# Side pieces of a state-space scan queued by an account of engine work, with depthwise taps as diagonal products on TensorE

## The chip, the cores and the metric

The kernel runs on one core of one Trainium2 chip. It uses TensorE (PE: matrix products into PSUM, with its weight load PEld), VectorE (DVE), ScalarE (ACT), GpSimd (POOL) and SyncE (SP, which here only issues DMAs). The metric is the device time of one execution in microseconds (us); lower is better. All tensors are float32.

## The reference

One layer works on x of shape (4, 256, 32, 32): four batches, 256 channels, 1024 tokens. Cut to what matters:

```python
xs = layernorm_over_channels(x)                      # twice, with and without weights
xc = xn split in 4 groups of 64 channels
xm = mamba(xc) + skip * xc                           # per group: u, z = xs @ inw.T; causal conv of 4 taps; silu;
                                                     # dt = softplus(...); h = exp(dt*A) * h + dt*u*B; y = sum_s h*C
g  = sigmoid(pointwise(grouped_conv3(xm)));  xg = g * xm
R   = pointwise(depthwise3(xg, rdw_w)) + xg
cat = concat(xs, R)
xm2 = pointwise(depthwise3(cat, fdw_w)) + xs
x_local, x_global = depthwise3(xm2, lc_w), mha(xm2)  # 8 heads of 32
xo = gelu(layernorm(concat(x_local, x_global) @ fc_w.T))
xi = depthwise3x3(ln_hw(xo), dwc_w)                  # 9 taps per channel on the 32 x 32 image
x  = x + proj(layernorm(xi))
t  = tokens of x;  t = t + top-2-of-8 experts(layernorm(t))   # 256 -> 1024 -> 256
```

## The kernel before, in words

Channels lie on the 128 partitions (two chunks `c` of 256 channels), tokens along the free dimension, in two halves `h` of 512. For each batch `b` there are eight *parts*: group `n` = 0 to 3, half `h` = 0 and 1; so parts 0, 2, 4, 6 are first halves and parts 1, 3, 5, 7 second halves. A part has 16 *steps*; a step scans 128 of the 128 x 16 pairs of channel and state, 32 channels x 4 states on the partitions.

`scan` writes the instructions of a step. In `step`, VectorE makes dBu (line 528) and scans it along 512 tokens (line 535); GpSimd keeps the last column in first halves (line 539) and multiplies by C (line 540). ScalarE makes the decay dA three steps ahead (line 521). TensorE makes the B rows of the next four steps (`spread_b`, line 513) and sums states of the last four (`sums_of`, line 546), each as four products on a quarter of the array. Tables `before`, `behind` and `group` say at which step the pieces of the part before, the part behind and the next group are written: state sums at step 1, `gather` at 3, `project_out` at 6, `add_skip` at 8.

The order of instructions on every engine is the order in which the program writes them (`manual_schedule`). All the rest of the layer is written as generators, the *side pieces*: `normalised` (layer norm of the next batch), `convolutions` (gate, three-tap convolutions, pointwise products, then values, queries and keys in `prepared`), `attention`, `local`, and `mixing` (output projection, `fc`, norm, GELU, the 3x3 convolution, norm, projection, then `dispatch`, which routes tokens to experts and scatters 16 row blocks with indirect DMAs, line 1423). After each step `beat` advances a clock by one, and each running generator, in the order of the list `running`, runs until its own due time lies ahead: `yield 1` means due again at the next beat, `yield 2` at the one after, `yield 0` now. `drain` beats without scans until no generator is left. `in_turn` writes a product for one item and, two items later, the use of an earlier one.

The program starts `convolutions(b-1)` at part 0 of batch b. It waits until step 9 of that part, when the batch's scans have all been gathered. After part 3 `drain` is called, then attention(b-1), with mixing(b-1) behind it, local(b-1) and normalised(b+1) are started; beats run without scans until the attention is nearly through; then parts 4 to 7 follow, with mixing beside them, and what is left of mixing and its `dispatch` goes on beside the next batch's part 0. The last batch's convolutions, attention and mixing run with no scan beside them.

A three-tap depthwise convolution (`depthwise3`) is one activation on ScalarE for the first tap (line 353) and two instructions on VectorE that multiply by a column of weights and add (line 358), each on 128 x 1024. The 3x3 one in `mixing` is an activation for the middle tap (line 1013) and eight such instructions per chunk (line 1021). `product` (line 325) is a pointwise convolution: chunks of 128 x 128 weights on 512 tokens. In the profile one float32 product shows as two records of matmul and two of weight load.

After the layer the routed tokens go through the experts in 39 tiles (lines 1510 to 1578), and the result is brought back.

Of the kernel before, what the change touches and what calls it, by code (L numbers as in the profile page):

```python
# [1 line left out]

# [7 lines left out]
F32 = mybir.dt.float32  # L10
# [4 lines left out]
P = 128  # L15
# [29 lines left out]

LOG_EXP = "natural_log_exp_and_others"


# [18 lines left out]
def network(  # L67
# [26 lines left out]
):  # L94
    nc = tc.nc
    shifted = sums is None
# [18 lines left out]
    def col(name, i=0, rows=slice(0, P)):  # L115
# [3 lines left out]
    ident = cpool.tile([P, P], F32, name="ident")  # L119
    make_identity(nc, ident)  # L120
    ones_mean = cpool.tile([P, P], F32, name="ones_mean")
# [12 lines left out]
        W1, W2, b2, out,  # L134
    )


    with tc.tile_pool(name="w_conv", bufs=1) as wp, tc.tile_pool(
# [88 lines left out]

        ones = wp.tile([P, P], F32, name="ones")
        nc.gpsimd.memset(ones, 1.0)

# [90 lines left out]
        def product(name, w, co, chunks):  # L321

            out = ps(name)
            for ci, chunk in enumerate(chunks):
                nc.tensor.matmul(
                    out, w[:, ci, ts(co, P)], chunk, start=(ci == 0), stop=(ci == len(chunks) - 1)
                )
            return out

        def column_mean(name, chunks):  # L330

            out = ps(name)
            for ci, chunk in enumerate(chunks):
                nc.tensor.matmul(
                    out, ones_mean, chunk, start=(ci == 0), stop=(ci == len(chunks) - 1)
                )
            return out

        def in_turn(items, make, use, lag=2):

            made = []
            for at in range(len(items) + lag):
                if at >= lag:
                    use(items[at - lag], made[at - lag])
                if at < len(items):
                    made.append(make(items[at]))
                yield 1
# [3 lines left out]
        def depthwise3(dst, c, src, c_src, w, wi, bias):  # L351

            nc.scalar.activation(
                dst[:, c, :], src[:, c_src, 0:N], AF.Identity, bias=bias, scale=col(w, 3 * wi)
            )
            yield 1
            for k in (1, 2):
                nc.vector.scalar_tensor_tensor(
                    dst[:, c, :], src[:, c_src, k : k + N], col(w, 3 * wi + k), dst[:, c, :],
                    ALU.mult, ALU.add,  # L360
                )
                yield 1

        LEFT = KC - 1
# [8 lines left out]
        def normalised(b):  # L373
# [20 lines left out]
            for h in range(2):  # L394
                sq = [a2(f"sq_{b}_{h}_{c}") for c in range(NC2)]
                for c in range(NC2):
                    nc.gpsimd.tensor_tensor(sq[c], part(c, h), part(c, h), ALU.mult)
                yield 1
                var = column_mean(f"var_{b}_{h}", sq)
                yield 2  # L400
                root(r1[:, half(h)], var, eps6)
                yield 1
                root(r2[:, half(h)], var, eps11, scale=1.0 + 1e-5)
                yield 1
# [104 lines left out]
        def spread_b(b, n, h, q):  # L509
            bs = T[b, n, h, "bs", q] = ps(f"bs_{b}_{n}_{h}_{q}")  # L510
            for i, r in enumerate(states):
                s = DTR + 4 * q + i
                nc.tensor.matmul(  # L513
                    bs[r], xpwT_s[:, n, s : s + 1].to_broadcast([P, 32]),
                    T[b, n, "u"][:, half(h)], start=True, stop=True,
                )
# [25 lines left out]
        def sums_of(b, n, h, q):  # L542
            if q == 0:
                T[b, n, h, "yp"] = ps(f"yp_{b}_{n}_{h}")
            for g in range(GD):
                nc.tensor.matmul(  # L546
                    T[b, n, h, "yp"][ts(g, 32)], quads, T[b, n, h, "hs", q * GD + g],
# [15 lines left out]
        def add_skip(b, n, h):  # L563
# [9 lines left out]
        before = {  # L573
            1: [(sums_of, GS - 1)], 3: [(gather,)], 6: [(project_out,)], 8: [(add_skip,)],
        }
# [44 lines left out]
        def scan(at, i, stop):  # L620
# [17 lines left out]
            if g == 0 and q + 1 < GS:  # L638
                spread_c(b, n, h, q + 1)
            if g == 1 and q > 0:  # L640
                sums_of(b, n, h, q - 1)
# [31 lines left out]
        def convolutions(b):  # L673
# [49 lines left out]
            for c in range(NC2):  # L723
# [3 lines left out]
                yield 1  # L727
            for c in range(NC2):
                yield from depthwise3(d[1], c, xm, c, "rdw_w", c, col("rdw_b", c))

# [11 lines left out]
            d[1] = a8(f"d4r_{b}")  # L742
            for c in range(NC2):
                yield from depthwise3(d[1], c, xm, c, "fdw_w", NC2 + c, col("fdw_b", NC2 + c))

# [84 lines left out]
        def attention(b):  # L830
# [12 lines left out]
            def logits(g, h, kt):  # L843
# [3 lines left out]
                for i in range(4):  # L847
                    r = ts(i, HD)
                    nc.tensor.matmul(  # L849
                        sts[i], k[r, ts(kt, P)], q[r, half(h)], start=True, stop=not shifted  # L850
# [14 lines left out]
            def sum_pair():  # L865
                kt, acc, es = pairs.pop()
                for i in range(4):
                    nc.tensor.matmul(
                        acc[ts(i, HD)], ones[:, 0:HD], es[i], start=(kt == 1), stop=(kt == NK - 1)
                    )  # L870
# [18 lines left out]
            for at, (g, h, kt) in enumerate(steps):  # L889
# [6 lines left out]
                for i in range(4):  # L896
                    nc.tensor.matmul(  # L897
                        accs[0][ts(i, HD)], v8[:, kt, ts(4 * g + i, HD)], es[i],
# [21 lines left out]
            for _ in ending.pop():  # L920
                yield 1

        def local(b):
# [8 lines left out]
        def mixing(b):  # L932
# [25 lines left out]
            def inverse_deviation(name):  # L958
# [8 lines left out]
                for h in range(2):  # L967
                    sq = squares(h)
                    yield 1
                    var = column_mean(f"var_{name}_{h}", sq)  # L970
                    yield 2
# [30 lines left out]
            xi = a8(f"xi_{b}")  # L1002
            xz = []
            for c in range(NC2):
                xz.append(
# [5 lines left out]
                )  # L1011

                nc.scalar.activation(
                    xi[:, c, :], xz[c].rearrange("p i j -> p (i j)"), AF.Identity,
                    bias=col("dwc_b", c), scale=col("dwc_w", 9 * c + 4),
                )
                yield 1
                for k in (0, 1, 2, 3, 5, 6, 7, 8):
                    acc = xi[:, c, :].rearrange("p (i j) -> p i j", j=WW)
                    (to_i, at_i), (to_j, at_j) = (edge(d - 1) for d in divmod(k, 3))  # L1020
                    nc.vector.scalar_tensor_tensor(
                        acc[:, to_i, to_j], xz[c][:, at_i, at_j], col("dwc_w", 9 * c + k),
                        acc[:, to_i, to_j], ALU.mult, ALU.add,
                    )
                    yield 1 if k % 2 else 0

            xc = xi
# [44 lines left out]

        def beat():

            nonlocal tick
            tick += 1
            for one_ in list(running):
                while one_[0] <= tick:
                    try:
                        one_[0] += max(next(one_[1]), 0)  # L1080
                    except StopIteration:
                        running.remove(one_)
                        break

        def drain():
# [11 lines left out]
        with tc.manual_schedule(engines=ALL):  # L1097
            log_exp()
            start(normalised(0), weights())
            drain()  # L1100
            first_part()
            for b in range(B):
                for p in range(PARTS):
# [6 lines left out]
                    for i in range(NSTEP):  # L1110
                        scan(at, i, stop)
                        if b > 0 and p == 0 and i == 9:
                            whole(b - 1)
                        beat()
                    if b > 0 and p == PARTS // 2 - 1:
# [7 lines left out]
                        while not T.get(("attended", b - 1)):  # L1123
                            beat()
                        resume(at + 1)
            start(finish_part(len(parts) - 1))
            drain()
# [33 lines left out]
class Experts:  # L1161
# [141 lines left out]
    def dispatch(self, b, X1, XR, root):  # L1303
# [116 lines left out]
        for j in range(2):  # L1420
            for t in range(NT):
# [8 lines left out]
                self.sent.append(ins)  # L1430
                yield 1

# [267 lines left out]
```

## Time and profile before

| | |
|---|---|
| time before, median of 3 | 2745.61 us (2745.22 to 2754.72) |
| the profiled execution's own time | 2743.95 us |
| its span | 2742.2 us, mean granted clock 0.893 |
| busy PE, PEld | 2179.7 us (79%), 983.5 us (36%) |
| busy DVE, ACT, POOL | 1736.6 (63%), 1164.7 (42%), 1142.1 us (42%) |
| batch 0's scans | 78.2 to 359.8 us |
| batch 1, 2, 3: parts 0 to 3 | 168.5, 190.7, 189.9 us |
| batch 1, 2, 3: attention without scans | 93.6, 92.4, 82.4 us |
| batch 1, 2, 3: parts 4 to 7 | 179.8, 178.9, 177.8 us |
| last batch's rest with no scan | 1713.8 to about 2040 us |
| experts | about 2040 to 2742 us |

The limits of parts are the starts of their first scan at line 535; after part 3 the attention's stretch begins 32.5 us after that part's first scan. A stretch's busy times say which engine was full in it; a busy PE is not PE at its peak, since matmuls are pipelined.

### The profile page before, as it was taken

Reading aid. Unit: us, or ns where it says so; the run is one execution under the profiler, and the core shown is the slowest. Engines: PE = TensorE matmul, PEld = TensorE weight load, DVE = VectorE, ACT = ScalarE, POOL = GpSimd, SP = SyncE. Lnnn points to the kernel's source line nnn. Section 1 sums busy time; section 2 is a strip of 40 time slices with the busy share of each in tenths; the row PEclk is TensorE's granted clock in tenths of the full one; section 3 lists DMA queues with packets and bytes.
Section 4 is the critical chain, followed back from the end, with each engine's and each line's share of the span. In section 5 each row is a group of like instructions: output and inputs, shape, how many; then the busy total and the mean of one; then the engine's idle time right before and its main releaser. Section 6 shows DMA issues by size and latency. Waiting matters only on the chain. (4 is left out here: it accounts for less than half of the span.)

```text
span 2742.2 us, 28466 instructions
## 1 busy us (share of the span) xinstructions
PE 2179.7 (79%) x9082; PEld 983.5 (36%) x9082; DVE 1736.6 (63%) x2413; ACT 1164.7 (42%) x1938; POOL 1142.1 (42%) x1171
## 2 busy tenths in 40 slices
PE   6677787999676899867689976599439998999972
PEld 2111112322121332212132211232128777777761
DVE  2789989778999887899987889437431211211211
ACT  2544544575554368545347662246312222222220
POOL 2677767425775742676671366300021111111112
PEclk8888988999888999989799997799769999999995
DMA  2434432302242320333321132100056554555526
GB/s 84 110 99 102 100 98 66 82 24 50 68 132 54 97 59 24 77 79 103 82 69 43 30 77 52 62 4 13 0 187 211 181 171 160 179 178 181 180 72 199
DMA packets 148839, 263.26 MB, mean 96 GB/s; under 512 B 28256, under 2 KB 94084, under 8 KB 147656
## 3 DMA queue, kind: packets, MB, share of 16 engines
q1 hardware_dynamic: 136240, 233.68, 29.9%
q0 software_dynamic: 7408, 20.35, 2.1%
q10 hardware_dynamic: 5032, 7.32, 0.8%
q8 instruction: 73, 1.20, 0.2%
q14 instruction: 86, 0.70, 0.1%
HBM read 159.39 MB, written 34.77 MB: 71 GB/s over the span
## 5 line engine op out<-in xcount | busy, mean ns | idle before, releaser
L540 POOL TENSOR_TENSOR hs<-hs,cs 128x512 f32<-128x512 f32 x512 | 689.2, 1347 | 205.0 <-DVE hs L535 154.5
L521 ACT ACTIVATE dA<-dts,A 128x512 f32<-128x512 f32 x512 | 343.0, 713 | 299.6 <-DMA dts<-dt 197.6
L546 PE MATMUL yp<-hs,quads 128*32 128x512 f32 x1024 | 315.4, 675 | 154.2 <-POOL hs L540 126.8
L528 DVE TENSOR_TENSOR dBu<-dts,bs 128x512 f32<-128x512 f32 x512 | 347.9, 680 | 41.5 <-DMA dts<-dt 24.2
L1559 ACT ACTIVATE hs<-h,b 128x256 f32<-128x256 f32 x312 | 147.9, 474 | 470.5 <-PE h L1555 470.5
L535 DVE TENSOR_TENSOR_SCAN hs<-dA,last,dBu 128x512 f32<-128x512 f32 x256 | 327.6, 1280 | 24.9 <-ACT sq_fin L964 0.5
L535 DVE TENSOR_TENSOR_SCAN hs<-dA,dBu 128x512 f32<-128x512 f32 x256 | 312.4, 1220 | 30.7 <-ACT dA L521 6.7
L1555 PE MATMUL h<-xT,w 128*128 128x256 f32 x1248 | 285.1, 387 | 43.8 <-DVE xT L1536 43.8
L1574 POOL DMA_INDIRECT Y<-ys,dest x78 | 74.6, 957 | 559.6 <-DVE ys L1573 367.7
L859 ACT ACTIVATE e<-st 128x512 f32<-128x512 f32 x512 | 264.8, 603 | 89.6 <-PE st L849 88.8
L1563 PE MATMUL y<-w,hs 128*128 128x256 f32 x1248 | 275.9, 379 | 0.0
L1555 PEld LDWEIGHTS h<-xT,w 128*128 128x128 f32 x1248 | 229.9, 192 | 92.6 <-DVE xT L1536 53.3
L1563 PEld LDWEIGHTS y<-w,hs 128*128 128x128 f32 x1248 | 237.1, 190 | 32.2
L513 PE MATMUL bs<-u,xpwT_s 128*32 128x512 f32 x1024 | 175.3, 676 | 60.1 <-DVE hs L535 50.7
L539 POOL COPY last<-hs 128x1 f32<-128x1 f32 x256 | 92.4, 361 | 299.9 <-DVE hs L535 292.7
L909 DVE TENSOR_TENSOR e<-e,e 128x512 f32<-128x512 f32 x256 | 167.1, 714 | 51.3 <-ACT e L859 26.7
L546 PEld LDWEIGHTS yp<-hs,quads 128*32 128x32 f32 x1024 | 51.8, 117 | 392.3 <-POOL hs L540 287.9
L849 PE MATMUL st<-qk 32*128 32x512 f32 x1024 | 173.9, 651 | 4.4 <-DVE hs L535 4.1
L1529 DVE TENSOR_REDUCE b<-mine 128x8 f32<-128x64 f32 x39 | 8.5, 219 | 263.5 <-ACT hs L1559 263.5
L430 PE MATMUL up<-xn,inwk 64*128 64x512 f32 x256 | 138.5, 688 | 26.3 <-DVE hs L535 19.6
L897 PE MATMUL av<-e,v 128*32 128x512 f32 x1024 | 142.1, 615 | 0.0
L1539 DVE TENSOR_SCALAR late<-xs,expert 128x2 f32<-128x2 f32 x39 | 8.9, 228 | 201.5 <-DMA xs<-XS 201.5
(267 smaller groups left out, 2679.9 us busy)
## 6 DMA issues: line engine op xcount, KB each, us to landing
w<-in_W_dram SPq DMA_DIRECT2D x78, 1024.0 KB, 5.5
dts<-dt SPq DMA_DIRECT2D x512, 128.0 KB, 2.4
cs<-cd SPq DMA_DIRECT2D x512, 64.0 KB, 2.1
xs<-XS SPq DMA_DIRECT2D x39, 260.0 KB, 5.0
yy<-Y SPq DMA_DIRECT2D x8, 1024.0 KB, 6.5
b<-in_b_dram SPq DMA_DIRECT2D x39, 128.0 KB, 5.0
xn<-in_x_dram SPq DMA_DIRECT2D x4, 1024.0 KB
XL<-xl SPq DMA_DIRECT2D x8, 512.0 KB, 2.8
```

What stands on the lines that cost most here:

```text
L513: nc.tensor.matmul(bs[r], xpwT_s[:, n, s : s + 1].to_broadcast([P, 32]), T[b, n, "u"][:, half(h)], start=True, stop=True,)
L521: nc.scalar.activation(dA, T[b, n, h, "dts", g][:, 0, :], AF.Exp, scale=A[:, g, n, q : q + 1])
L528: nc.vector.tensor_tensor(dBu, T[b, n, h, "dts", g][:, 1, :], T[b, n, h, "bs", q], ALU.mult)
L535: nc.vector.tensor_tensor_scan(hs, T[b, n, h, "dA", i], dBu, 0.0 if h == 0 else last, ALU.mult, ALU.add)
L540: nc.gpsimd.tensor_tensor(hs, hs, T[b, n, h, "cs", q], ALU.mult)
L546: nc.tensor.matmul(T[b, n, h, "yp"][ts(g, 32)], quads, T[b, n, h, "hs", q * GD + g], start=(q == 0), stop=(q == GS - 1),)
L849: nc.tensor.matmul(sts[i], k[r, ts(kt, P)], q[r, half(h)], start=True, stop=not shifted)
L859: nc.scalar.activation(es[i], sts[i], AF.Exp, scale=1.0 / HD**0.5)
L909: nc.vector.tensor_tensor(first[i], first[i], es[i], ALU.add)
L1555: nc.tensor.matmul(hp[:, i, :], w1[:, c, ts(k, P)], xT[:, c, :], start=(c == 0), stop=(c == NC2 - 1),)
L1559: nc.scalar.activation(hs[:, k, :], hp[:, i, :], AF.Gelu, bias=b1_s[:, k, :])
L1563: nc.tensor.matmul(yp[:, ts(t, C)], hs[:, k, ts(t, P)], w2[:, k, :], start=(k == 0), stop=(k == NHC - 1),)
```

## The change

Each engine gets a `Meter`: whenever the program names an instruction of that engine, a fixed price is added to its account. Products on a quarter of the array go to a meter of their own, a quarter of which is charged to TensorE. While scans run, `beat` goes on with side pieces only as long as neither TensorE nor ScalarE nor GpSimd stands more than 1.0 above VectorE's account; an account never falls more than 2.0 below it. The rule holds in all of batch 0, in parts 0 to 3, and after the attention is over; in a drain and while attention runs without scans it does not. `product` and `column_mean` become generators that may be interrupted after each product. The taps of `rdw_w`, of the second half of `fdw_w` and of the 3x3 convolution become TensorE products with diagonal matrices, made by ScalarE; those of the first half of `fdw_w` and of `local` stay as they were. State sums move from step 1 to 2 and from g == 1 to g == 2, `gather` from step 3 to 4, scatters to every second beat. `ones` is the experts' tile of ones.

```diff
+class Meter:
+    def __init__(self, engine, cost):
+        self.engine, self.cost, self.us = engine, cost, 0.0
+
+    def __getattr__(self, name):
+        self.us += self.cost.get(name, 0.0)
+        return getattr(self.engine, name)
...
+        self.vector = Meter(nc.vector, {
+            "tensor_tensor": 0.7, "tensor_tensor_scan": 1.25, "scalar_tensor_tensor": 1.0,
+            "tensor_copy": 0.2, "tensor_scalar": 0.3, "tensor_reduce": 0.3, "bn_stats": 0.6,
+            "bn_aggr": 0.2, "reciprocal": 0.2,
+        })
+        self.scalar = Meter(nc.scalar, {"activation": 0.7, "copy": 0.6})
+        self.gpsimd = Meter(nc.gpsimd, {
+            "tensor_tensor": 1.4, "tensor_scalar": 2.0, "tensor_copy": 0.35,
+            "indirect_dma_start": 1.0,
+        })
+        self.tensor = Meter(nc.tensor, {"matmul": 0.86, "transpose": 0.25})
+        self.quarter = Meter(nc.tensor, {"matmul": 0.86})
...
-    nc = tc.nc
+    nc = Metered(tc.nc)
...
+    experts.nc = nc
...
-        ones = wp.tile([P, P], F32, name="ones")
-        nc.gpsimd.memset(ones, 1.0)
+        ones = experts.every
...
                     out, w[:, ci, ts(co, P)], chunk, start=(ci == 0), stop=(ci == len(chunks) - 1)
                 )
+                yield 0
             return out
...
+        def depthwise3_pe(name, dst, src, w, at, bias):
+            diags = []
+            def diagonals(c):
+                for k in range(3):
+                    diags.append(small.tile([P, P], F32, tag="diag", name=f"dg_{name}_{c}_{k}", bufs=4))
+                    nc.scalar.activation(
+                        diags[-1], ident, AF.Copy, scale=col(w, 3 * (at + c) + k)
+                    )
+            def taps(item):
+                c, h = item
+                out = ps(f"{name}_{c}_{h}")
+                for k in range(3):
+                    nc.tensor.matmul(
+                        out, diags[3 * c + k], src[:, c, ds(k + h * HALF, HALF)],
+                        start=(k == 0), stop=(k == 2),
+                    )
+                if item == (0, 1):
+                    diagonals(1)
+                return out
+            diagonals(0)
+            yield 1
+            yield from in_turn(
+                CO_H, taps,
+                lambda item, out: nc.scalar.activation(
+                    dst[:, item[0], half(item[1])], out, AF.Identity, bias=col(bias, at + item[0])
+                ),
+            )
...
         before = {
-            1: [(sums_of, GS - 1)], 3: [(gather,)], 6: [(project_out,)], 8: [(add_skip,)],
+            2: [(sums_of, GS - 1)], 4: [(gather,)], 6: [(project_out,)], 8: [(add_skip,)],
         }
...
-            if g == 1 and q > 0:
+            if g == 2 and q > 0:
                 sums_of(b, n, h, q - 1)
...
-            for c in range(NC2):
-                yield from depthwise3(d[1], c, xm, c, "rdw_w", c, col("rdw_b", c))
+            yield from depthwise3_pe(f"rd_{b}", d[1], xm, "rdw_w", 0, "rdw_b")
...
-            for c in range(NC2):
-                yield from depthwise3(d[1], c, xm, c, "fdw_w", NC2 + c, col("fdw_b", NC2 + c))
+            yield from depthwise3_pe(f"fd1_{b}", d[1], xm, "fdw_w", NC2, "fdw_b")
...
             for _ in ending.pop():
                 yield 1
+            T["over", b] = True
+            level()
...
+            order = [(c, k) for c in range(NC2) for k in (4, 0, 1, 2, 3, 5, 6, 7, 8)]
+            def taps(at):
+                for c, k in order[at : at + 1]:
+                    if k == 4:
+                        banks[c] = [ps(f"dw_{b}_{c}_{h}") for h in range(2)]
...
+                    for h in range(2):
...
+                        nc.tensor.matmul(
...
+                            diags[c, k], xz[c][:, lo + move : hi + move, at_j],
+                            start=(k == 4), stop=(k == 8),
+                        )
...
-                for k in (0, 1, 2, 3, 5, 6, 7, 8):
-                    acc = xi[:, c, :].rearrange("p (i j) -> p i j", j=WW)
-                    (to_i, at_i), (to_j, at_j) = (edge(d - 1) for d in divmod(k, 3))
-                    nc.vector.scalar_tensor_tensor(
-                        acc[:, to_i, to_j], xz[c][:, at_i, at_j], col("dwc_w", 9 * c + k),
-                        acc[:, to_i, to_j], ALU.mult, ALU.add,
-                    )
-                    yield 1 if k % 2 else 0
+            diagonals(2)
+            for at in range(len(order)):
+                taps(at)
+                diagonals(at + 3)
+                yield 0
+                if at % 9 == 8:
+                    c = at // 9
+                    yield 2
+                    for h in range(2):
+                        nc.scalar.activation(
+                            xi[:, c, half(h)], banks[c][h], AF.Identity, bias=col("dwc_b", c)
+                        )
...
-        def beat():
+        def beat(beside=False):
             nonlocal tick
             tick += 1
+            others = (nc.tensor, nc.scalar, nc.gpsimd)
+            nc.tensor.us += nc.quarter.us / 4
+            nc.quarter.us = 0.0
+            for engine in others:
+                engine.us = max(engine.us, nc.vector.us - 2.0)
             for one_ in list(running):
-                while one_[0] <= tick:
+                while one_[0] <= tick and not (
+                    beside and max(e.us for e in others) > nc.vector.us + 1.0
+                ):
                     try:
                         one_[0] += max(next(one_[1]), 0)
...
+        def level():
+            for engine in (nc.tensor, nc.scalar, nc.gpsimd):
+                engine.us = nc.vector.us
...
-                        beat()
+                        beat(beside=not b or p < PARTS // 2 or T.get(("over", b - 1)))
...
                         resume(at + 1)
+                        level()
...
                 self.sent.append(ins)
-                yield 1
+                yield 2
```

## The prediction, made before the change was run

> **What bounds the kernel now.** I read the 40 slices of the page first, then busy time by stretch, cut at the first scan of each part (DVE line 535), then the groups by form, then the timeline of one crowded part and of the stretch after the last scan. The chain that ended last is no help: it holds only the last 4 us.
>
> ```profile
> PE   6677787999676899867689976599439998999972
> DVE  2789989778999887899987889437431211211211
> PEclk8888988999888999989799997799769999999995
> ```
>
> Up to about 1700 us VectorE (DVE) is nearly full and TensorE is not far behind; then comes a stretch with neither full, and from 2040 us the experts, which the change does not touch. A stretch's columns are length, then busy time of PE, PEld, DVE, ACT, POOL, then clock:
>
> ```profile
> 294.50:326.40 31.90, 26.49 (x88) 6.45 (x88) 30.25 (x34) 18.48 (x27) 26.36 (x36) 0.95 0.42 103
> 326.40:359.80 33.40, 22.98 (x73) 3.98 (x72) 31.47 (x35) 13.91 (x22) 24.21 (x20) 0.93 0.41 99
> ...
> 852.70:908.70 56.00, 32.10 (x100) 8.35 (x98) 54.28 (x67) 21.75 (x31) 40.04 (x43) 0.76 0.28 75
> 908.70:959.90 51.20, 43.06 (x140) 16.54 (x138) 39.89 (x43) 21.93 (x33) 38.14 (x50) 0.93 0.32 85
> 959.90:992.40 32.50, 31.19 (x119) 10.99 (x117) 31.05 (x33) 19.48 (x32) 23.61 (x19) 0.96 0.35 85
> ...
> 1171.00:1225.80 54.80, 35.33 (x85) 9.61 (x81) 53.22 (x57) 22.39 (x31) 42.09 (x35) 0.75 0.28 72
> ```
>
> The first two are parts (16 scan steps) with no side work: three such, 33.1, 31.9 and 33.4, average 32.8 us, nearly all of it dBu and scan. The others carry side pieces of batch 0 or 1. At 1171 (the 3x3 taps) VectorE has 53 of 54.8 us busy; at 908 (pointwise products) it is idle 11 us, of which its residuals wait 9.7 us for line 325's products. So the parts are held by VectorE in one place and by TensorE's order in another.
>
> ```profile
> 1659.41 2.48 DVE L1021 SCALAR_TENSOR_TENSOR xi<-xz,V,xi 128x961 f32<-128x961 f32 x2
> 1660.73 2.29 POOL L540 TENSOR_TENSOR hs<-hs,cs 128x512 f32<-128x512 f32 x1
> 1661.81 0.69 DVE L528 TENSOR_TENSOR dBu<-dts,bs 128x512 f32<-128x512 f32 x1
> 1662.53 1.22 DVE L535 TENSOR_TENSOR_SCAN hs<-dA,dBu 128x512 f32<-128x512 f32 x1
> ```
>
> One step costs 0.69 + 1.22 of VectorE, and two taps beside it 2.48: the taps double the step. (GpSimd's product takes 2.29 beside them, 1.27 alone, but is not last.)
>
> **The taps, one by one.** Removed per batch: 4 + 4 taps of line 358 at 1.26 and 16 of line 1021 at 1.24, 30 us of VectorE. Added: 12 + 12 + 36 products of 512 columns. A product is two records; these rows show its price (first row warm, last row from a cold start), the quarter products' (second) and the 3x3's in the tail:
>
> ```profile
> 1798.88 1.45 PE L325 MATMUL fp<-d4r,fpwT_s 128*128 128x512 f32 x3
> ...
> 1683.03 1.06 PE L513 MATMUL bs<-u,xpwT_s 128*32 128x512 f32 x8
> ...
> 1952.44 20.17 DVE L1021 SCALAR_TENSOR_TENSOR xi<-xz,V,xi 128x961 f32<-128x961 f32 x16 [2.58 <-ACT xi L1013]
> 1972.76 4.68 PE L334 MATMUL mean<-xi,ones_mean 128*128 128x512 f32 x6 [8.00 <-DVE xi L1021]
> 1985.80 9.00 PE L325 MATMUL pr<-xi,projT_s 128*128 128x512 f32 x16 [2.70 <-DVE xi L976]
> ```
>
> Three warm records take 1.45, the last of them 0.59 (the shortest at line 325), so they start 0.43 apart: 0.86 a product, 51.6 us of TensorE per batch for 30 us of VectorE. Diagonals (128x128 on ScalarE) have no row: between 0.21 (128x8, line 1368) and 0.60 (128x512, line 859); I take 0.3, as the shape is nearer the first: 30 of them 9 us (6 to 18), and 12 evictions of 0.69, 8 us, less 6 activations of 1.24: 10 us more a batch (7 to 19) on an engine that is half idle in these stretches, hidden by the three decays queued ahead (6 us of scan); behind a diagonal that waits for its buffer (four, freed by the taps) stand the decays, and for them the scans; if that cover goes, each such wait costs its length. The 3x3 also holds two PSUM banks over nine taps where it held none; with bs two, yp, dBu and up's two, all eight are taken in a first half: between 0 and one step (2 us) each time, I take 0.
>
> **The account.** In what follows "priced" is the diff's own cost table. Per part VectorE is priced 16 x 1.95 + 2 x 1.0 = 33.2. GpSimd is priced 19 x 1.4 = 26.6, and in first halves another 16 x 0.35 = 32.2: headroom 1.0 in a first half, 6.6 in a second. TensorE's own work is 32 quarter products / 4 x 0.86 = 6.9 plus 12 or 4 full ones, 13.8 on average: headroom 19.4, or 22 products a part. A side piece is queued only while all three stand below VectorE + 1.0, and unused headroom beyond 2.0 is lost. From this I can place every piece:
>
> Batch 1, parts 0 to 3 (side: batch 0's convolutions, 96 priced products). From step 9 of part 0 there are 3.4 parts x 22 = 75 products, and 12 side taps and residuals on VectorE are priced 12 us, 14 more, less a few lost in waits: some 11 products are left when part 3 ends, and the drain runs them with no scan beside. 4 x 32.8 + 4 taps 5.1 + 8 residuals 5.9 + residuals behind their products 9 (before: 9.7 in one part) + drain 11 x 0.86 = 9.5: 161 to 164, against 168.5 before. Take -5.
>
> Parts 4 to 7 of batches 1 and 2 (side: end of attention, then mixing with 8 + 16 + 4 + 36 + 4 + 4 + 8 = 80 products, 3.6 parts of headroom). The last mean, variance and projection slip into the next batch's part 0, with xr's load and XD's store on SP; these pass only spreads of dts and cs (2.4 and 2.1 us to landing), among which they stood before: 0. 131 + end blocks 8.4 (39.6 busy less a clean 31.2) + bn and lgn 5 + a wait of 5 for the first inverse deviation, now queued without its spacing + 6 since four quarter products really take 1.06 (line 513) where 0.86 is priced, eight times a part: 156, against 179.8 and 178.9: -24 and -23. This is the gain.
>
> Batches 2 and 3, parts 0 to 3: the step that decides. dispatch's 16 scatters are priced 1.0 each on GpSimd. By the account they start at step 3 of part 1, and what GpSimd has from there is 8 (3 from floor to limit, 13 x 0.55 + 2.0 - 4.2) + 1.0 + 6.6 = 15.6, against 16 scatters and two gate products of 1.4. Mixing stands ahead of convolutions in the list of running pieces, so each bit of headroom goes to a scatter, and the max over engines stops the convolutions too. They stand at the gate from part 1, through two parts with scans alone, until the drain after part 3. There 64 products of 0.86 and 16 of 0.43 (256 columns) run with VectorE idle: 62 us. Time: 131 + leftover centring, scaling and residuals 8 + dispatch 13 + 4 taps 5 + waits 10 + 62 = 229, against 190.7 and 189.9: +38 and +39. The waits: a piece that was held comes due several times over and is queued in one go (mean, squares, variance and root in one beat, where line 970 once waited two); behind the scaling on VectorE stand dBu and scan, and for them GpSimd and TensorE wait. In the tail mean to scaling takes 1984.52 - 1972.76 = 12 us; TensorE runs some 2 us ahead, so I take 10, between 0 and 12.
>
> Parts 4 to 7 of batch 3: mixing finishes inside: 156 + 8 + 9 of such waits = 173, against 177.8: -5. After the last scan dispatch follows as before: 0.
>
> Tail (batch 3, nothing beside): the convolutions were 55 us from line 724 (1769.5) to the first logits (1824.8); now 12 + 8 + 12 + 16 + 16 products and 16 half ones follow one another, 72 x 0.86 = 62, and a first eviction and residual: 64, +9. The 3x3 was 20.2 on VectorE; now 36 x 0.86 = 31.0, +2.0 for a cold start (line 325's 16 records take 9.00, warm ones 15 x 0.43 + 0.59 = 7.0), +1.4 evictions, less about 2 as the mean then finds the array warm: +12. Sum +21.
>
> The Trainium skill's TensorE: Matmul & The Clock Gate (What's actually happening) has the array at half rate until about 3.4 us of sustained work; by it the cold start would be worth half of that, 1.7 us, not 2.0, and the sum 0.3 less.
>
> Sums moved one step later (steps 2 and 4, g == 2) let the TensorE queue stand less behind GpSimd (PE's waits of 126.8 us at line 546), mostly idle time off the path: -2 in batch 0, between -10 and 0. Scatters at every second beat: between -16 (their own 16 x 1.0) and 0; 0, as GpSimd is not last in those parts (38 of 51 busy). ones from the experts' tile: the same matrix, 0.
>
> Sum: -2 - 5 - 24 + 38 - 23 + 39 - 5 + 21 = +39 on 2743.95, the profiled execution's own time (span 2742.2 and 1.75 around it); it lies 1.7 under the median of 2745.61, so 2785. Uncertain are the two drains, the three stretches of parts 4 to 7 and the tail by 8 each, in square 20, and the waits by up to 10 a batch, 30 for three: 36 together.
>
> **Rivals.** *Faster:* the convolutions of batches 1 and 2 do get their turns, so drains stay short. For it: VectorE idles 18 us in those four parts before and loses 10 us of taps. Price: both +38 become -5: 2744 - 2 - 5 - 24 - 5 - 23 - 5 - 5 + 21 = 2696, 2698 at the median. It decides if rd's diagonal products of batch 1 are queued before part 3 of batch 2 ends. Against it: 15.6 of headroom for 18.8. *Much slower:* TensorE becomes the bound in parts 4 to 7, where the account keeps it as full as VectorE while its in-order queue still waits at line 546 for GpSimd: a part takes 39 instead of 35 to 37, the 24 + 23 + 5 us of gain go, 2837. *No change:* gains in parts 4 to 7 of some 36 each cancel the drains, about 2745.
>
> **How the numbers follow.** About 0.5%, 14 us, is what a measurement here can tell. Chances: forecast 0.55, much slower 0.10, no change 0.11, faster 0.24. So slower 0.65, same 0.11, faster 0.24. The range reaches down to 2688, ten under the faster case, and up to the much slower one; the forecast's own range is 2750 to 2820.
>
> **What would show it.** Right: batch 2 and 3's parts 2 and 3 take about 33 us each with almost no line 325, then some 60 us with TensorE full and no line 535; parts 6 of 55 us become about 36; L1021 gone, its time in the tail 31 to 35 us. Wrong: rd products beside scans in batch 2 (then the faster case), or parts 4 to 7 above 39 us (then the much slower one).

## The result and the profile after

The changed kernel takes 2822.47 us (median of 4 runs, 2815.76 to 2835.08) against 2745.41 for the kernel before, timed alternately: a ratio of 1.0283, 95% interval 1.0234 to 1.0331. The forecast was 2785 with a range of 2688 to 2840: the sign and the places were right, the size was 37 us short, and the forecast's own case (2750 to 2820) ended 2 us below what came. The profiled execution took 2815.76 us (span 2814.0), against 2743.95 (2742.2) before.

The 40 slices of its page show two new holes in VectorE (DVE): 5 and 3 tenths in slices 14 and 15 and 2 in slice 22, where it stood at 8, 8 and 7 before, with TensorE (PE) at 7, 9 and 9:

```profile
PE   6767779998978799898679988599747999999982
DVE  2888898689977537997862798418231111121111
PEclk8887789999977799997879999799978999999995
```

Busy time by stretch, columns as before (length, then PE, PEld, DVE, ACT, POOL, clock). The first line is a part 6 of batch 1, the next four are parts 0 to 3 of batch 2, the last the stretch after them, with no scan:

```profile
697.30:734.30 37.00, 31.95 (x99) 11.03 (x99) 32.46 (x39) 22.75 (x38) 25.84 (x35) 0.86 0.33 80
767.40:831.10 63.70, 52.40 (x175) 21.72 (x176) 45.17 (x62) 27.48 (x42) 26.71 (x38) 0.76 0.38 106
831.10:886.30 55.20, 40.51 (x114) 8.64 (x107) 44.54 (x82) 23.30 (x35) 29.51 (x32) 0.75 0.24 61
886.30:926.40 40.10, 33.14 (x88) 8.47 (x89) 30.42 (x35) 18.65 (x28) 30.23 (x42) 0.66 0.38 99
926.40:958.90 32.50, 21.45 (x69) 4.87 (x63) 30.69 (x33) 13.04 (x25) 29.76 (x32) 0.79 0.41 106
958.90:1025.00 66.10, 59.35 (x150) 28.90 (x148) 6.15 (x9) 14.46 (x26) 6.76 (x8) 0.95 0.08 27
```

Part 6, 54.8 us before, is 37.0. Part 3 has nothing beside its scans (32.5), and 66 us of products follow with VectorE at 6 us. Parts 0 and 1 take 63.7 and 55.2 with about 45 us of VectorE each: it is idle for 29 us in the two. The pointwise products of the same stretches (line 359: length, PE, PEld) say who was held. Part 0 has the 16 records of the last projection; in parts 1 to 3 there is none:

```profile
767.40:831.10 63.70, 7.93 (x16) 2.71 (x16) 0.76 0.38 106
831.10:886.30 55.20, 0.00 (x0) 0.00 (x0) 0.75 0.24 61
886.30:926.40 40.10, 0.00 (x0) 0.00 (x0) 0.66 0.38 99
926.40:958.90 32.50, 0.00 (x0) 0.00 (x0) 0.79 0.41 106
958.90:1026.00 67.10, 34.83 (x80) 15.16 (x80) 0.95 0.08 26
```

In the tail the 3x3 is now these products (TensorE's timeline, start and length):

```profile
2017.98 32.01 PE L1094 MATMUL dw<-xz,dg 128*128 128x512 f32 x72 [9.28 <-ACT dg L1081]
2049.83 3.60 PE L369 MATMUL mean<-xi,ones_mean 128*128 128x512 f32 x8
```

By stretch, in the two profiled executions (starts of the first scans; "to part 4" holds the attention's stretch too):

| stretch | before | after | difference | forecast |
|---|---|---|---|---|
| batch 0 | 281.6 | 284.9 | +3 | -2 |
| batch 1, part 0 to part 4 | 262.1 | 251.1 | -11 | -5 |
| batch 1, parts 4 to 7 | 179.8 | 153.1 | -27 | -24 |
| batch 2, part 0 to part 4 | 283.1 | 350.4 | **+67** | **+38** |
| batch 2, parts 4 to 7 | 178.9 | 151.8 | -27 | -23 |
| batch 3, part 0 to part 4 | 272.3 | 340.8 | **+68** | **+39** |
| batch 3, parts 4 to 7 | 177.8 | 160.5 | -17 | -5 |
| last scan to the end | 1028.4 | 1043.1 | +15 | +21 |
| sum | | | +72 | +39 |

### The profile page after: what moved, and what is told of

Its sections match the earlier page's. It is cut to its first block, busy times and chain, and to the rows that moved or that the text cites. A ratio compares the mean times of both kernels' runs of the same rounds, so it can differ in the third digit from the quotient of the medians.

```text
span 2814.0 us, 29508 instructions
## 1 busy us (share of the span) xinstructions
PE 2331.2 (83%) x9562; PEld 1067.1 (38%) x9562; DVE 1590.9 (57%) x2317; ACT 1205.0 (43%) x2082; POOL 1055.4 (38%) x1170
## 5 line engine op out<-in xcount | busy, mean ns | idle before, releaser
L609 POOL TENSOR_TENSOR hs<-hs,cs 128x512 f32<-128x512 f32 x512 | 650.5, 1274 | 221.8 <-DVE hs L604 176.3
L615 PE MATMUL yp<-hs,quads 128*32 128x512 f32 x1024 | 242.7, 690 | 53.1 <-POOL hs L609 48.4
L499 PE MATMUL up<-xn,inwk 64*128 64x512 f32 x256 | 170.6, 824 | 8.1 <-POOL xn L481 6.8
L608 POOL COPY last<-hs 128x1 f32<-128x1 f32 x256 | 51.2, 200 | 321.1 <-DVE hs L604 314.6
L916 PE MATMUL st<-qk 32*128 32x512 f32 x1024 | 163.9, 638 | 0.2
L1094 PE MATMUL dw<-xz,dg 128*128 128x496 f32 (+3 forms) x288 | 135.6, 620 | 14.9 <-ACT dg L1081 14.9
L615 PEld LDWEIGHTS yp<-hs,quads 128*32 128x32 f32 x1024 | 39.5, 117 | 230.8 <-POOL hs L609 127.2
```

The source lines that it names most:

```text
L499: nc.tensor.matmul(up, inwk[rows, c, k, :], XN[b][rows, c, ds(k + h * HALF, HALF)], start=(k == 0), stop=(k == KC - 1),)
L609: nc.gpsimd.tensor_tensor(hs, hs, T[b, n, h, "cs", q], ALU.mult)
L615: nc.quarter.matmul(T[b, n, h, "yp"][ts(g, 32)], quads, T[b, n, h, "hs", q * GD + g], start=(q == 0), stop=(q == GS - 1),)
L916: nc.quarter.matmul(sts[i], k[r, ts(kt, P)], q[r, half(h)], start=True, stop=not shifted)
```

## The experiments

The theory: mixing's last pieces (norm, projection, dispatch) are held by the account and come out bunched in parts 0 and 1; its scatters, priced on GpSimd, then hold the convolutions at the gate's multiplication (line 793) until the drain. Two columns make a quick test of it in each kernel: the time from the first scan of part 0 to that of part 3 of batch 2 (bunching and waits), and from there to part 4 (32.5 us of scans, the drain, then attention).

Medians and ratios are against the kernel before as timed beside each (2744.74 to 2751.99); the stretches are from one profiled execution each.

| kernel | median us | ratio to before, 95% | part 0 to 3 | part 3 to 4 |
|---|---|---|---|---|
| before | 2745.41 | 1 | 158.2 | 124.9 |
| after | 2822.47 | 1.0283 [1.0234, 1.0331] | 159.0 | 191.4 |
| e1, scatters free | 2718.42 | 0.9867 [0.9833, 0.9901] | 159.6 | 136.4 |
| e2, taps alone | 2703.76 | 0.9825 [0.9782, 0.9867] | 151.2 | 124.9 |
| e3, account alone | 2715.45 | 0.9867 [0.9836, 0.9899] | 147.7 | 130.0 |
| e4, e1 and mixing's end not held | 2674.25 | 0.9709 [0.9679, 0.9740] | 143.5 | 134.4 |
| e5, moved steps alone | 2764.67 | 1.0068 [1.0040, 1.0095] | 161.6 | 125.4 |
| e6, e4 with the tail's taps on VectorE | **2657.47** | 0.9665 [0.9636, 0.9694] | 143.6 | 134.3 |
| e7, 3x3 on VectorE | 2775.51 | 1.0106 [1.0075, 1.0136] | 140.4 | 162.1 |
| e8, e6 with the old steps | 2690.49 | 0.9787 [0.9758, 0.9815] | 150.3 | 134.6 |
| e9, after with the old steps | 2819.36 | 1.0266 [1.0239, 1.0293] | 162.1 | 191.6 |
| e10, e4 with scatters priced | 2680.99 | 0.9759 [0.9726, 0.9792] | 142.4 | 134.1 |
| e11, only the 3x3 on TensorE | 2801.91 | 1.0208 [1.0173, 1.0243] | 159.0 | 184.7 |

**e1: the scatters' price.**

```diff
-            "indirect_dma_start": 1.0,
+            "indirect_dma_start": 0.0,
```

> The changed kernel with one number changed: an indirect DMA is priced 0 instead of 1.0 on GpSimd's account. Theory (the scatters eat GpSimd's headroom, so the convolutions are held until the drain): by the account the convolutions of batches 1 and 2 then run beside parts 1 to 3 as batch 0's do, and 11 instead of 80 products are left for each drain; the stretches of 66 us between part 3 and the attention shrink to about 9, parts 2 and 3 of batches 2 and 3 become like batch 1's (38.6 and 35.7 us instead of 40.1 and 32.5). 2 x 56 us less than 2822: about 2710, between 2680 and 2740. Rival (TensorE has too much work with the diagonal products, wherever they stand): the 69 products a batch only lengthen parts 1 to 3 by their 59 us; within 40 us of 2822.

Measured 2718, as the theory said. One number in a table of prices turns a loss of 2.8% into a gain of 1.3%. It takes 55 us out of part 3 to part 4 and nothing out of parts 0 to 3, whose waits must have another cause.

**e2 and e3: each half by itself.** e2 puts only the diagonal products into the kernel before, with no account (the 3x3 yields a beat after each tap):

```diff
-                yield from depthwise3(d[1], c, xm, c, "rdw_w", c, col("rdw_b", c))
+            yield from depthwise3_pe(f"rd_{b}", d[1], xm, "rdw_w", 0, "rdw_b")
```

> The kernel before with the diagonal products alone: no account, no steps moved, a beat after each tap of the 3x3 (two products). Theory (the taps themselves gain where scans stand beside them, and lose some 15 us in the tail): part 6 of 55 us loses 20 us of VectorE, parts 1 and 2 of each batch 10, and TensorE, at 2 x 0.86 and 0.96 a step beside the 3x3, gives back some 13 in parts 6 and 7: 3 x 17 less and 15 more, about 2710, between 2680 and 2745. Rival (the diagonal products are what makes the changed kernel slow): 2790 or more.

Measured 2704, as expected. e3 is the other half: the changed kernel with every tap as it was before.

```diff
-            yield from depthwise3_pe(f"rd_{b}", d[1], xm, "rdw_w", 0, "rdw_b")
+                yield from depthwise3(d[1], c, xm, c, "rdw_w", c, col("rdw_b", c))
```

> The changed kernel with all its taps on VectorE again, the account and the moved steps kept. Theory (the account's order is the loss): the drains of batches 2 and 3 stay, at some 50 us with 24 products fewer, part 6 is back at 55 us, the tail is back by 15 us: 2822 - 15 - 2 x 15 + 3 x 18 = about 2830, between 2790 and 2850. Rival (the diagonal products are the loss): about 2745.

This failed: 2715, not 2830. So the account with its priced scatters does not lose by itself: each half gains, and only together do they lose. The products at line 359 of e3's parts 1 to 3 and of the start of its drain show them queued all along:

```profile
833.30:897.30 64.00, 10.35 (x16) 3.54 (x16) 0.79 0.24 64
897.30:937.60 40.30, 10.95 (x21) 4.50 (x22) 0.83 0.37 94
937.60:970.10 32.50, 14.56 (x33) 5.79 (x32) 1.00 0.38 99
970.10:985.00 14.90, 5.14 (x12) 1.90 (x11) 1.00 0.39 115
```

**e7 and e11: which half of the taps holds the convolutions.** e7 is the changed kernel with only the 3x3 back on VectorE, e11 with only the three-tap ones back.

```diff
# e7
-                        nc.tensor.matmul(
...
-                            diags[c, k], xz[c][:, lo + move : hi + move, at_j],
+                    nc.vector.scalar_tensor_tensor(
+                        acc[:, to_i, to_j], xz[c][:, at_i, at_j], col("dwc_w", 9 * c + k),
# e11
-            yield from depthwise3_pe(f"fd1_{b}", d[1], xm, "fdw_w", NC2, "fdw_b")
+                yield from depthwise3(d[1], c, xm, c, "fdw_w", NC2 + c, col("fdw_b", NC2 + c))
```

> The changed kernel with the 3x3 alone back on VectorE; diagonal products of the three-tap convolutions, account and moved steps as changed. Theory (it is the account's order that decides, not the products): mixing then ends some 14 steps earlier, the gate of the convolutions is through before the scatters begin, and by the account 51 and 57 products are left for the drains of batches 2 and 3 instead of 80, some 45 us instead of 66; parts 0 lose their 20 us of waits, parts 6 are back at 55 us: 2822 - 2 x 36 + 3 x 18 - 10 = about 2795, between 2770 and 2815. Rival (the 3x3 on TensorE is the whole loss): 2750 or less.

> The changed kernel with the three-tap taps (rdw and the second half of fdw) back on VectorE; only the 3x3 stays as diagonal products. It asks why e3, with all taps on VectorE, had drains of some 4 products. Theory (the 3x3 on TensorE makes mixing late, its scatters then stand ahead of the gate products, and the convolutions are held before a single tap is named): drains of batches 2 and 3 stay at 40 to 60 us, taps in them at VectorE's pace: about 2790 (2765 to 2810). Rival (the taps' own price of 1.0 each on VectorE's account lets the convolutions go): drains under 15 us, about 2720.

Measured 2776 and 2802, both within what was expected. The same products in e11's parts 1 to 3 and drain are as in the changed kernel:

```profile
831.00:886.30 55.30, 0.00 (x0) 0.00 (x0) 0.75 0.23 63
886.30:926.30 40.00, 0.00 (x0) 0.00 (x0) 0.62 0.39 97
926.30:958.80 32.50, 0.00 (x0) 0.00 (x0) 0.82 0.43 106
958.80:1018.00 59.20, 38.84 (x79) 16.14 (x80) 0.84 0.10 30
```

Part 3 to 4 falls from 191 to 185 with the three-tap taps on VectorE, to 162 with the 3x3 there, and to 130 with both. With the 3x3 on TensorE the convolutions are held before they reach a tap; with it on VectorE (e7) the taps of rdw_w and all 16 records of the first pointwise product run in parts 1 and 2, and then they are held, 64 records of line 359 being left. That with both on VectorE they are not, since each tap they name adds 1.0 to VectorE's account, follows from the diff; no run shows that by itself.

**e4 and e10: mixing's end not held.** From the end of its 3x3 to the end of dispatch, mixing is queued as in the kernel before: whatever the accounts say, and due from the beat in which it last ran, so that nothing comes due twice. e4 has the scatters free as in e1, e10 has them priced again.

```diff
-                while one_[0] <= tick and not (
-                    beside and max(e.us for e in others) > nc.vector.us + 1.0
+                while one_[0] <= tick and (
+                    (T.get("loose") and one_[1] is T.get("chain")) or not (
+                        beside and max(e.us for e in others) > nc.vector.us + 1.0
+                    )
                 ):
...
+                        if T.get("loose") and one_[1] is T.get("chain"):
+                            one_[0] = tick + wait
```

> The first of these kernels (scatters priced 0), and mixing is not held any more from the end of its 3x3 on, so its last norm, projection and dispatch keep the beats between their pieces. Theory (pieces that were held come due all at once, and VectorE waits behind them): parts 0 and 1 of batches 2 and 3, 119 us together with VectorE idle for 29, become about 100, and part 7 of batch 3 loses some 8: 40 to 50 us less than the kernel with scatters priced 0, about 2665, between 2640 and 2700. Rival (parts 0 and 1 are long because TensorE is busy 52 of 64 us there): within 10 us of the kernel with scatters priced 0.

> The kernel of e4 with the scatters priced at 1.0 again: mixing is not held by the account from the end of its 3x3 to the end of dispatch, but its scatters still load GpSimd's account. Theory (two causes, one behind the other): the waits of parts 0 and 1 are gone as in e4 (their sum 96, against 120 in the changed kernel), but the 16 scatters still put GpSimd's account so far ahead that the convolutions are held, and the drains of batches 2 and 3 stay at 40 to 66 us: about 2745 (2725 to 2775). Rival (the waits alone held everything; once dispatch comes early, the price does no harm): drains under 20 us, about 2680.

e4 came as expected. e10 did not: the rival was right, with 2681 instead of 2745. Once mixing's end runs at its own pace, the scatters' price does little or no harm: the intervals of e4 and e10 overlap, and both profiled executions span 2679. In e10 the products at line 359 in parts 1 to 3 are:

```profile
817.10:869.40 52.30, 9.44 (x20) 3.55 (x18) 0.90 0.34 89
869.40:916.40 47.00, 9.81 (x17) 3.30 (x18) 0.93 0.25 63
916.40:948.90 32.50, 14.47 (x31) 5.19 (x30) 1.00 0.43 109
```

The first of its 16 scatters starts at 901.3 and the last at 957.7; in the changed kernel it is 862.2 and 962.9. So it is not that dispatch comes early, as the expectation had it, but that while mixing is spaced the convolutions pass the gate beside it, with its multiplications at 835 and 839, before the first scatter. The hold on mixing's end is the root; the price only decides whether the drain follows from it. The edit frees norm, projection and dispatch together; no run frees one of them alone, and none puts the convolutions ahead of mixing in the list.

**e6: the last batch's taps on VectorE**, everything else as in e4.

```diff
-            yield from depthwise3_pe(f"rd_{b}", d[1], xm, "rdw_w", 0, "rdw_b")
+            if b < B - 1:
+                yield from depthwise3_pe(f"rd_{b}", d[1], xm, "rdw_w", 0, "rdw_b")
+            else:
+                for c in range(NC2):
+                    yield from depthwise3(d[1], c, xm, c, "rdw_w", c, col("rdw_b", c))
```

> Scatters priced 0 and mixing not held after its 3x3, as in the kernel of that name, and the last batch, which has no scans beside it, keeps its taps on VectorE. Theory (in the tail the diagonal products follow one another on TensorE, 60 of them, where VectorE's 24 taps were shorter): the stretch from the last scan to the experts loses 15 to 21 us: about 2657, between 2645 and 2668. Rival (the tail is set by something else, diagonal products are hidden there): within 5 us of 2674.

Measured 2657. From part 4 of batch 3 to the end e6 takes 14 us less than e4 (1192.5 against 1206.3), so the products cost about that much where no scan stands beside them, a little less than the 15 to 21 expected. This is the fastest version, 3.35% under the kernel before.

**e5, e8, e9: the moved steps.** e5 is the kernel before with the move alone; e8 and e9 are e6 and the changed kernel without it.

```diff
-            1: [(sums_of, GS - 1)], 3: [(gather,)], 6: [(project_out,)], 8: [(add_skip,)],
+            2: [(sums_of, GS - 1)], 4: [(gather,)], 6: [(project_out,)], 8: [(add_skip,)],
...
-            if g == 1 and q > 0:
+            if g == 2 and q > 0:
```

> The kernel before with the moved steps alone: state sums at step 2 and g == 2, gather at step 4. Theory (idle time of TensorE's queue off the path): -2 in batch 0 and at most some 10 in all, 2735 to 2748. Rival (the moved steps, not the account, are what made the account without diagonal products 30 us faster than before): about 2715.

> The kernel of e6 with the state sums and gather back at their old steps (1, g == 1, 3). Theory: e5's loss is the moved steps themselves. Its parts 4 and 6 of batch 0 took 37.5 and 37.4 us, against 33.3 and 31.9 before, and in them VectorE waits 4.0 us for a decay that follows a late dt; after and e6 have the same two parts at 37.5. So both go back to about 33 (9 us), and some 5 to 10 us come from the crowded parts of batches 1 to 3 as in e5: about 2642 (2632 to 2650), parts 4 and 6 of batch 0 under 34.5. Rival: the old steps make TensorE's queue stand behind GpSimd's products again where side pieces now fill TensorE (line 546 of before); then batch 0 gains 9 and batches 1 to 3 lose as much: 2657 (2652 to 2668).

> The changed kernel with the state sums and gather back at their old steps (1, g == 1, 3) and all else kept. Theory (the moved steps cost what e5 shows, 19 us): about 2805 (2795 to 2815), with parts 4 and 6 of batch 0 at 33 instead of 37.5. Rival (the move only pays beside the account): batches 1 to 3 lose more than batch 0's 9 us, and the time is 2822 or more.

e5 failed: 19 us slower, where -11 to +2 was expected. The waits of part 4 of batch 0, which has nothing beside it, show how (engine, line, what it waited for: us in all, times, longest):

```profile
PE op L561 <- POOL y L556: 5.3, 1, 5.3
...
DVE hs L535 <- ACT dA L521: 4.0, 1, 4.0
ACT dA L521 <- DMA dts<-dt: 3.9, 1, 3.9
```

GpSimd's product `y` is queued a step later, `op` on TensorE waits for it, the next part's input products stand behind `op`, so its dt is stored and loaded late and the first decay too. Parts 4 and 6 take 37.5 and 37.4 instead of 33.3 and 31.9, in the changed kernel likewise 37.5. These two parts are 10 of the 15 us that batch 0 loses in e5's profile; 7 more lie in its part 2, of which the last section tells, and part 0 is 3 shorter. With the old steps e8 and e9 have them back at 32.0 to 33.3; but e8 is 33 us slower than e6, not 15 faster, and e9 (2819) came neither to the 2805 of its theory nor to the 2822 of its rival: it stays within the interval of the changed kernel. The move costs alone, costs nothing in the changed kernel, and pays beside spaced side pieces. In e8 the loss lies in the crowded parts (part 1 of batch 2 takes 61.5 us, in e6 53.0, with VectorE busy 43.4 and 43.7). There dBu waits 9.0 us for the gate's sigmoid and 5.3 for the eviction of rd, the products of the rdw_w taps; in e6 it is 2.5 and 2.8. Why the old steps lengthen these waits stays open.

## Why the prediction was right, and where it was short

**Right: the gate and the drain.** After the gate's own products (842.5 to 860 us, in part 1) batch 2 holds no product of the convolutions until TensorE runs ahead into those of the drain at 954, and the drains of batches 2 and 3 take 66.1 and 66.7 us where 62 was worked out from 64 products of 0.86 and 16 of 0.43. The shortage of headroom was real, as e1 shows from the price and e10 from the hold. Its size was right too: by the order on GpSimd in batch 2, 14 of the 16 scatters and one of the two gate multiplications (1.4) come before the last scan's product of part 3, 15.4 by price, where 15.6 had been worked out.

**Right: parts 4 to 7.** -27 and -27 for -24 and -23: part 6 falls from 54.8 to 37.0 as the 3x3 leaves VectorE. The "much slower" rival, by which TensorE would have eaten that gain, is out. One sign was badly set: the forecast's 156 us are 39 a part, the very mark above which it was to be wrong, while the rival's price, the whole gain gone, means 45. Measured are 38 a part. In batch 3 it is -17 instead of -5: of the 17 us put there for dispatch's pieces and their waits, 160.5 against batch 2's 151.8 leaves 9.

**Right: the tail.** +15 for +21. The 72 records of the 3x3 take 32.0; 36 x 0.86 = 31.0 and 2.0 for a cold start had been put down. From the end of the variance to the end of the mean the time grows from 35.1 to 44.6, 9.5 where 12 was said.

**The step that was mis-sized: "waits 10" a batch in parts 0 to 3, with "0 to 12".** VectorE's busy time there was right: 150.8 us in the four parts of batch 2, while the sum's clean parts (123.4 busy of 131.7) plus 26 of pieces make 149.4. Its idle time is 40.7 us, where 8 in the clean parts and 10 were allowed. VectorE's own waits in parts 0, 1 and 2 give 27.8 of it:

```profile
DVE d L395 <- ACT d L390: 7.7, 1, 7.7
DVE xi L1045 <- ACT r_fin L353: 4.6, 1, 4.6
...
DVE dBu L597 <- ACT g L786: 7.8, 1, 7.8
...
DVE hs L604 <- ACT dA L590: 4.4, 1, 4.4
DVE dBu L597 <- PE bs L582: 3.3, 1, 3.3
```

The 4.6 in part 0 is the norm's chain that had been costed. The other three had not:

- `convolutions` loads xl and comes due four beats later. Held by the account behind mixing, it starts with its due time long past: the load is issued at 790.4, the first use on ScalarE follows in the same beat and waits 7.7 us for it, the tap behind it on VectorE stands as long, and dBu and scan behind the tap. The four beats of lead were not in the working.
- The gate's products yield a beat after every three; with all beats already owed they go in one go, and a dBu stands behind them:

```profile
842.51 13.21 PE L759 MATMUL qd<-xm,qdwT_s 128*4 128x512 f32 x24
855.65 4.59 PE L776 MATMUL gp<-qs,qpwT_s 4*128 4x512 f32 x8
...
857.75 1.27 ACT L786 ACTIVATE g<-gp,V 128x512 f32<-128x512 f32 x2
858.47 0.69 DVE L597 TENSOR_TENSOR dBu<-dts,bs 128x512 f32<-128x512 f32 x1 [7.79 <-ACT g L786]
```

  These are 17.8 us of TensorE. dBu starts as the first of the two sigmoids ends, and before the next B rows (860.19), so it does not wait for B rows. It reads nothing that the sigmoid writes; what is left is its buffer, one of the eight in PSUM that all products and dBu share. Waits for these buffers had been put at 0, for the 3x3 alone. That pieces held come "due several times over" stood in the prediction, but was counted for the norm alone. In e10, where mixing's end is not held, parts 0 and 1 have no wait of VectorE longer than 2.6 us.
- 4.4 and 3.3 us in part 2 are in part the moved steps' late dt and what follows from it, the waits of e5; with the old steps (e9) 2.5 and 1.7 are left there. The step "mostly idle time off the path: -2" was wrong in sign by itself. In the changed kernel's sum it does little: with the old steps part 2 is 36.2 instead of 40.1, and part 0 71.9 instead of 63.7.

Of the 29 us that batch 2's stretch is above its term, 23 are this idle time, 4 the drain (66.1 for 62) and 1 VectorE's work. The two stretches came out 58 us above their +38 and +39, the other terms together 26 us below, so that errors of both signs partly cancelled by luck: 33 on the sum, and the rest of the 37 is how the profiled executions lie to the medians.

**The "faster" rival** had the right price: e1, e4 and e10, in which the convolutions get their turns, give 2718, 2674 and 2681, and it had said 2698. Its turning point, whether rd's products are queued before part 3 of batch 2 ends, does not hold in general: in e7 all of them run in part 1 (869.8 to 882.1), the convolutions are held behind them, and the time is 2776. How near the edge 15.6 of headroom for 18.8 was, no run shows; e1 frees 16, five times what was missing.

## What to carry to other kernels

An account that holds a list of pieces by the fullest engine lets the first piece in the list starve all others; a long chain with priced instructions at its end should be spaced, not held, and two edits that each gain can lose together through the order of that list. When a piece is held, its due times must move with it, or its loads lose their lead and its products come in one burst ahead of the critical ones. Where no work stands beside it, work should not be moved away from an engine that is otherwise idle: the last batch deserves a form of its own.

## What was not expected of the hardware

TensorE stayed at half rate through some 25 us of unbroken work in eight of the thirteen profiled executions. Part 2 of batch 0 took 38.8 us before, 39.4 after, and 38.9 to 39.7 in e3, e7 and e11, but 46.1 to 48.8 in the other eight. The edits do not explain it: e2 took 47.6 there, and its batch 0 is that of the kernel before but for the tile of ones. TensorE's timeline after its wait for GpSimd's `sq`, of the changed kernel:

```profile
164.69 3.78 PE L369 MATMUL var<-sq,ones_mean 128*128 128x512 f32 x4 [4.76 <-POOL sq L466]
168.41 3.89 PE L499 MATMUL up<-xn,inwk 64*128 64x512 f32 x8
172.22 1.06 PE L582 MATMUL bs<-u,xpwT_s 128*32 128x512 f32 x8
```

and of e8:

```profile
167.22 3.78 PE L369 MATMUL var<-sq,ones_mean 128*128 128x512 f32 x4 [3.34 <-POOL sq L466]
170.93 7.19 PE L499 MATMUL up<-xn,inwk 64*128 64x512 f32 x8
178.05 1.93 PE L582 MATMUL bs<-u,xpwT_s 128*32 128x512 f32 x8
...
190.45 1.93 PE L615 MATMUL yp<-hs,quads 128*32 128x512 f32 x8
192.31 2.44 PE L369 MATMUL var<-sq,ones_mean 128*128 128x512 f32 x4
194.59 1.02 PE L529 MATMUL dtp<-u,wdt 128*128 128x512 f32 x2
```

The first four records cost 3.78 in both. Then one is at full rate, 3.89 and 1.06, while the other goes on at about half of it, 7.19 and 1.93, until some 25 us after its start; the part's granted clock is 0.87 in the one and 0.65 in the other, and 0.50 in e8 from 167.2 to 192.3. The Trainium skill's TensorE: Matmul & The Clock Gate (What's actually happening) releases the clock after one busy window of about 3.4 us; the first trace agrees, the second does not. It is worth 7 to 9 us here, so single parts of two profiled executions should not be compared more closely than that.

The thirteen traces do show where the two kinds part. Around here the granted clock changes only after whole multiples of 3.41 us, so that time falls into steps. In the five executions of the first kind one step had TensorE busy for at least 87% of it, and 71 to 97% of the step was the four products of `var`, which fill all 128 rows and columns; the clock doubled at the end of that step. In the other eight the steps cut `var` in two: it filled 56 to 81% of one step, with TensorE idle ahead of it, and 28 to 53% of the next. Four or five steps more then passed at a clock of 0.50, although TensorE was busy from end to end with products on 64 rows (`up`) and on quarters of the array, before the one at whose end the clock doubled. So busy time alone did not release it here. That the place of the steps against `var` decides is read from these traces; no run moved it on purpose.
